# Attention scores of a graph layer: a second of seven products split again, and one list of accumulator banks

## The chip, the cores and the metric

The kernel runs on one NeuronCore of a Trainium2 chip. What counts is the time of one execution on the device, in microseconds (us). TensorE (PE in the profile) multiplies into accumulator banks of 128 x 512 fp32; VectorE (DVE) and ScalarE (ACT) copy, add and reduce; GpSimdE (POOL) and SyncE (SP) mostly issue DMA transfers.

## What is computed

Two layers of a graph network over N = 4096 nodes with 512 features, all in fp32. The second, cut to what matters here:

```python
h = x @ edge_w
e = h @ h.T                                  # 4096 x 4096 scores
e = jnp.where(adj > 0, e, NEG_BIG)
edge_att = jax.nn.softmax(e, axis=1)
output = adj * (node_att * edge_att) @ (x @ weight) + bias
x = layernorm(x + output)
```

The first layer is `layernorm(x + relu(adj @ (sign0(x) @ sign(w).T)))`. `adj` is symmetric in where it is nonzero, and `h @ h.T` is symmetric, so a tile of scores is made once and also turned (transposed) for its mirror tile.

## The kernel before

The span of the profile has five stages: the first layer's aggregation (0 to about 480 us, `acc` at L459 and L460), a short transition to 510, `h` and its like by Strassen's seven products (L101, to 602), the **score stage** (602 to 1067), and the aggregation of the second layer with its finish (L1288, then L1438, to 1909). The change lies in the score stage, and in how its buffers pass on to the aggregation.

In the score stage the 4096 x 4096 scores are cut into tiles of 512 x 512. A `Single` (L723) makes one tile by plain matmuls (`pe`, L742). A `Couple` (L766) makes two tiles side by side: rows A and columns B, B+1, that is 512 x 1024. There are twelve couples in three groups, which share their columns within a group: `couples(4, 2, 3, 0, 1)`, `couples(6, 2, 3, 0, 1, 4, 5)` and `couples(2, 0, 1)` (L1598 to L1600), with singles ahead of each group and seven after the last.

A couple is one step of the Strassen-Winograd scheme, in which a 2 x 2 block product costs seven block products (m = 0 to 6) instead of eight. `operands` (L777) prepares the left sums s1 to s4 and, once a group, the right sums t1 to t4, all on DVE. The left sums of every second couple lie in a buffer of their own (`self.sums`, L801) out of the list `free` of score slots.

- `quad(q)` (L868) makes six of the seven products for two of the four row strips (q = 0 or 1). Each product is two matmuls of 128 x 128 by 128 x 512 that follow each other in one accumulator, and the products m = 0, 5, 6, 3 go into the bank `y` one onto the other, with a copy by ScalarE after each (L902, L907, L915, L920: c11, c12, c22, c21). Products 4 and 2 go into the bank `z`: after m = 4 DVE adds z to c22 (L916), and after m = 2 it adds z to c12 (L925).
- `second` (L832) makes the product m = 1, l12 by r21, for both strips at once. It takes a further step of the same scheme: seven products of 128 x 128 by 128 x 256 (L841), added into the score strips by DVE (L844 to L863). For it `second_left` makes four sums of 128 x 128 (L826 to L829), and `second_right` four differences of 128 x 256 once a group, which lie in half a `lent` buffer (`keep`).

Each step of these functions ends in `between()`, which runs a `tick` (L579): at most one turn of a finished strip on TensorE (transposes at L704, a copy by ScalarE at L705) or the like, one or two statistics rows on DVE (L665, 0.69 us, and L666, 1.2 us for 1024 columns) and exponentials on ScalarE (L675). A row of statistics needs a mask: 512 KB of adjacency that SP loads (L650) into a free half of a `lent` buffer, if `between` finds more than two free halves. So these pieces of work stand between the products in a fixed order on each engine. A strip is written to HBM by a DMA from POOL (L895) and then released.

The main loop interleaves the parts of one couple with the second `quad` of the couple before (`rest_`): one `next` is one stretch up to a `yield`. The order on each engine is that of the program.

There are eight PSUM banks: six of the pool `ps_mm`, handed out in turn by the tile framework whenever a tile is made (`pe`, `seven`, `inner`), and two of `ps_tr` for transposes. Where a bank is taken again, the new matmul waits until the last reader of the old contents is done; so it does where a matmul writes a part of a bank of which another part is still read. After the score stage the six banks are put into a list, `banks`, which the aggregation uses.

Of the kernel before, what the change touches and what calls it, by code (L numbers as in the profile page):

```python
# [11 lines left out]
F32 = mybir.dt.float32  # L12
# [6 lines left out]
P = 128  # L19
# [10 lines left out]
def kernel(  # L30
# [13 lines left out]
    nc = tc.nc  # L44
# [3 lines left out]
    W = 512  # L48
    NG = N // W
    BG = W // P  # L50
# [515 lines left out]
    lent = [(t, t[:, : BG // 2, :], t[:, BG // 2 :, :]) for t in lent]  # L566
    free = deque(slots_p.tile([P, BG, W], F32, name=f"slot{n}") for n in range(6))
    free_h = deque(h for t in lent for h in t[1:])

    free_e = deque(pan.tile([P, W], F32, name=f"line{n}", bufs=1) for n in range(6))  # L570


    now = [0]
# [149 lines left out]
    class Single:  # L723
# [7 lines left out]
        def main(self, between):  # L731
            A, B = self.A, self.B
            s = Uses(BG + 1 if self.diag else 3 * BG)
            if self.diag:
                self.mirror.t = s
            elif self.stays:
                kept_tiles[A, B] = s.buf
            for i in range(BG):
                lo = i if self.diag else 0
                pe = ps_mm.tile([P, W], F32, name="pe", tag="mm")  # L740
                for k in range(KD):
                    nc.tensor.matmul(  # L742
                        pe[:, lo * P :],
                        hT[:, k, ts(A * BG + i, P)],
                        hT[:, k, (B * BG + lo) * P : (B + 1) * W],
                        start=(k == 0),
                        stop=(k == KD - 1),
                    )
                    if k == KD - 1 or k % 2 and not (self.diag and i > 1):
                        between()  # L750
                src = s.buf[:, i, :]
                nc.scalar.copy(src[:, lo * P :], pe[:, lo * P :])
                turns.append((now[0] + 3, lambda i=i, s=s, src=src: self.mirror.turn(s, src, i)))
                if not self.diag:
                    stats.append((self.here.ready, 1, lambda i=i, s=s, src=src: self.here.row(i, s, src)))

                    if self.stays:
                        continue

                    def store(i=i, s=s, src=src):  # L760
                        nc.gpsimd.dma_start(s_d[A][B // 2][:, i, B % 2, :], src)
                        s.used()

                    stats.append((at_once, 0, store))

    class Couple:  # L766
# [10 lines left out]
        def operands(self):  # L777
            A, B, h = self.A, self.B, KD // 2
            if B not in Couple.right:
                r11, r12 = (hT[:, :h, ts(c, W)] for c in (B, B + 1))  # L780
                r21, r22 = (hT[:, h:, ts(c, W)] for c in (B, B + 1))
                t1, t2, t3, t4 = (lopp.tile([P, h, W], F32, name="right", tag="lop") for _ in range(4))
                nc.vector.tensor_sub(t1, r12, r11)
                nc.vector.tensor_sub(t2, r22, t1)
                nc.vector.tensor_sub(t3, r22, r12)
                nc.vector.tensor_sub(t4, r21, t2)
                Couple.right[B] = r11, r21, r22, t4, t1, t2, t3
                Couple.inner_right[B] = self.second_right(r21)
            low, high = (hT[:, f : f + h, ts(A, W)].rearrange("p k (q u w) -> p k q u w", u=2, w=P) for f in (0, h))
# [6 lines left out]
            else:  # L796
                self.sums = Uses(1)
                s2, s1, s3, s4 = (
# [6 lines left out]
            self.left = l11, l12, s4, l22, s1, s2, s3  # L805
            self.inner_left = self.second_left(l12)
            self.rows11, self.written = [None] * 2, [None] * 2

# [11 lines left out]

        def second_left(self, l):

            (l11, l12), (l21, l22) = ([l[:, k, q, :] for k in range(2)] for q in range(2))
            self.inner_sums = Uses(1, free_h)
            s1, s2, s3, s4 = (self.inner_sums.buf[:, 0, ts(n, P)] for n in range(4))
            nc.vector.tensor_add(s1, l21, l22)  # L826
# [5 lines left out]
        def second(self, between):  # L832

            left, (right, keep) = self.inner_left, Couple.inner_right[self.B]
            w = W // 2
            c11, c12 = (self.rows11[0][:, c] for c in (slice(w), slice(w, W)))
            x, y = (ps_mm.tile([P, W], F32, name="inner", tag="mm") for _ in range(2))
            u, v, z = x[:, :w], y[:, :w], y[:, w:]
# [19 lines left out]
            nc.vector.tensor_add(self.rows11[0], self.rows11[0], y)  # L858
            self.written[0]()
            between()  # L860
            yield
            multiply(u, 3)
            nc.vector.tensor_add(c21, c21, u)  # L863
            self.inner_sums.used()
            keep.used()
            yield

        def quad(self, q, between):  # L868

            left, right = self.left, Couple.right[self.B]  # L870
            y, z = (ps_mm.tile([P, W], F32, name="seven", tag="mm") for _ in range(2))
            strips = [Uses(4, free_h) for _ in range(2)]
            (c11, c12), (c21, c22) = ((s.buf[:, 0, :], s.buf[:, 1, :]) for s in strips)
            self.rows11[q] = c11

# [32 lines left out]
            between()  # L908
            if q:
                yield  # L910
            multiply(z, 4, True)
# [8 lines left out]
            nc.scalar.copy(c21, y)  # L920
            between()
            if not q:
                yield
            multiply(z, 2)
            nc.vector.tensor_add(c12, c12, z)  # L925
            if q:
                written(0)
            written(1)
            between()
            yield  # L930


    banks = deque()

# [6 lines left out]
    def panel(A):  # L941
# [6 lines left out]
        yield  # L948
        pt = banks.popleft() if banks else ps_tr.tile([P, W], F32, name="ptm", tag="tr")
        for i in range(BG):  # L950
# [6 lines left out]
                stop=True,  # L957
# [6 lines left out]
        nc.scalar.copy(mrow, pt)  # L964
        if banks:
            banks.append(pt)
# [660 lines left out]
    for n, u in enumerate(runs):  # L1627
# [10 lines left out]
        quads = [[c.quad(q, between) for q in range(2)] for c in u]  # L1638
        inners = [c.second(between) for c in u]
        for k, c in enumerate(u):  # L1640
            first, second = quads[k]
            rest_ = quads[k - 1][1] if k else None
            next(first)
            if rest_:
                next(rest_)
            next(first)
            if rest_:
                next(rest_)
                if u[k - 1].sums:
                    u[k - 1].sums.used()  # L1650
# [8 lines left out]
            next(inner_)  # L1659
            next(first)  # L1660
            next(inner_)
            next(second)
            next(inner_)
            next(second)
        next(rest_ := quads[-1][1])
        next(rest_)
        if u[-1].sums:
            u[-1].sums.used()
# [5 lines left out]
    todo = deque()  # L1674
    banks.extend(ps_mm.tile([P, W], F32, name=f"bank{n}", tag="mm") for n in range(6))
    plan = deque(p for n, u in enumerate(blocks) for p in u.order(in_two(n)))
# [137 lines left out]
```

## Time and profile before

| What | us |
|---|---|
| time, median of 3 runs (lowest, highest) | 1912.76 (1912.59, 1913.26) |
| the profiled execution | 1911.35 |
| its span, first to last instruction | 1909.4 |
| score stage, 602 to 1067: PE busy | 463.5 of 465 |
| the same: DVE busy | 313.3 |
| the same: ACT busy | 314.5 |
| aggregation and finish, 1067 to 1909: PE busy | 835.3 of 842 |
| the same: DVE busy | 702.5 |

The granted TensorE clock is 0.999 over the span. An instruction's row gives its start, its length, the engine, the line, its output and inputs; a bracket after it tells how long the engine had been idle and what released it. A fp32 matmul of the program appears as two records, "x4" are thus two matmuls. Lengths of matmul records overlap those of the next, so the spacing of starts says what a matmul costs. DVE records overlap too, by about 0.08 us.

### The profile page before, as it was taken

The page shows a single profiled execution, that of the slowest core. Times are in us where ns is not written, and L with a number is a line of the kernel's source. Part 1 is how long each engine was busy: PE and PEld are TensorE (multiplying, and loading weights), DVE is VectorE, ACT ScalarE, POOL GpSimd, SP SyncE. Part 2 cuts the span into 40 slices and gives each one's busy share as a digit, 9 for nine tenths or more (in the row PEclk, how much of TensorE's full clock was granted, in tenths as well). Part 3 has the DMA queues.
Part 4 walks back from the last instruction along what each step waited for, and adds up shares of the span by engine and source line. Part 5 has one row for each costly group of instructions (what it writes and reads, how often), then busy time and mean ns, then how long its engine had stood idle before and what let it go on. Part 6 is the DMA issues. An engine that isn't in the chain of part 4 may idle for free.

```text
span 1909.4 us, 20692 instructions
## 1 busy us (share of the span) xinstructions
PE 1897.1 (99%) x6886; PEld 1234.3 (65%) x6886; DVE 1457.4 (76%) x2237; ACT 1028.8 (54%) x1653; POOL 311.3 (16%) x449
## 2 busy tenths in 40 slices
PE   9999999999999999999999999999999999999998
PEld 6888888888644555555555556666666666666646
DVE  7777677776866567686864887898879988898947
ACT  6433333333212567666767666666676567657632
POOL 0133132231421111110110111111111111110100
PEclk9999999999999999999999999999999999999999
DMA  9889899898585378577784877887777877787731
GB/s 323 300 323 359 301 347 323 326 358 307 183 305 203 125 290 320 186 257 273 293 319 155 320 288 289 287 297 286 271 280 282 293 279 275 267 313 256 283 119 56
DMA packets 143915, 520.95 MB, mean 273 GB/s; under 512 B 15040, under 2 KB 15040, under 8 KB 136128
## 3 DMA queue, kind: packets, MB, share of 16 engines
q1 hardware_dynamic: 64368, 235.43, 36.0%
q0 software_dynamic: 67632, 248.54, 34.1%
q10 hardware_dynamic: 11808, 35.66, 5.1%
q8 instruction: 54, 0.88, 0.2%
q14 instruction: 53, 0.43, 0.1%
HBM read 397.93 MB, written 121.63 MB: 272 GB/s over the span
## 4 chain that ended last, share of the span: by engine, by line
PE 88%; DVE 6%; DMA 2%; issue 1%; ACT 1%; POOL 0%; ACTq 0%; DVEq 0%; POOLq 0%
PE bank L1288 33%; PE seven L878 12%; PE acc L459 11%; PE acc L460 11%; PE pe L742 6%; PE seven L101 5%; PE po L1438 4%; PE pt L704 3%; PE inner L841 2%; DVE slot L1057 1%; PE acc L253 1%; PE acc L255 1%; PE pt L419 1%; PE pw L228 1%; DVE lent L1057 1%
## 5 line engine op out<-in xcount | busy, mean ns | idle before, releaser
L1288 PE MATMUL bank<-lent,lop 128*128 128x256 f32 (+1 forms) x1496 | 483.0, 473 | 0.1
L1288 PEld LDWEIGHTS bank<-lent,lop 128*128 128x128 f32 x1496 | 283.9, 190 | 166.9 <-issue 140.1
L459 PE MATMUL acc<-xw,hi 128*128 128x512 f32 x960 | 376.6, 392 | 0.0
L460 PE MATMUL acc<-xw,lo 128*128 128x512 f32 x960 | 374.0, 390 | 0.0
L1288 PE MATMUL bank<-slot,lop 128*128 128x512 f32 (+1 forms) x800 | 286.4, 503 | 1.0 <-DVE slot L1069 0.8
L449 ACT CAST hi<-at 128x1024 fp32r<-128x1024 f32 x120 | 126.4, 1053 | 203.0 <-PE acc L459 151.1
L1288 PEld LDWEIGHTS bank<-slot,lop 128*128 128x128 f32 x800 | 151.6, 190 | 115.4 <-issue 100.9
L1299 ACT COPY over<-bank 128x512 f32<-128x512 f32 x200 | 115.9, 585 | 201.7 <-PE bank L1288 198.1
L460 PEld LDWEIGHTS acc<-xw,lo 128*128 128x128 f32 x960 | 180.4, 188 | 36.7 <-DVE lo L451 0.2
L459 PEld LDWEIGHTS acc<-xw,hi 128*128 128x128 f32 x960 | 180.3, 188 | 36.7
L451 DVE TENSOR_TENSOR lo<-at,hi 128x1024 fp32r<-128x1024 f32 x120 | 148.2, 1235 | 65.3 <-ACT hi L449 64.9
L666 DVE CUSTOM_DVE_ANT_0 line<-lent,slot 128x512 f32<-128x512 bf16 x140 | 90.2, 686 | 55.0 <-ACT slot L705 29.0
L742 PE MATMUL pe<-hT 128*128 128x512 f32 (+3 forms) x384 | 132.1, 486 | 0.0
L675 ACT ACTIVATE line<-line,nmax_c 128x512 f32<-128x512 f32 x160 | 114.7, 722 | 21.2 <-DVE nmax_c L666 20.8
L1450 DVE SCALAR_TENSOR_TENSOR xb<-po,f,xb 128x256 f32<-128x256 f32 x84 | 40.3, 481 | 75.0 <-PE po L1438 70.8
L742 PEld LDWEIGHTS pe<-hT 128*128 128x128 f32 x384 | 64.6, 191 | 41.4 <-issue 33.8
L1057 DVE CUSTOM_DVE_ANT_1 lent<-lent,line 128x2048 f32<-128x2048 f32 x39 | 88.7, 2284 | 0.0
L1261 ACT COPY bank<-over 128x512 f32<-128x512 f32 x144 | 86.7, 603 | 0.0
L704 PEld LDWEIGHTS pt<-ident,lent 128*128 128x128 f32 x418 | 52.4, 141 | 44.8 <-issue 34.8
L1060 ACT ACTIVATE lent<-lent 128x2048 f32<-128x2048 f32 x39 | 74.9, 1920 | 8.5 <-DVE lent L1057 8.2
L705 ACT COPY slot<-pt 128x512 f32<-128x512 f32 (+3 forms) x123 | 68.3, 557 | 12.3 <-PE pt L704 12.2
L420 ACT COPY x1T<-pt 128x512 f32<-128x512 f32 x32 | 18.7, 585 | 101.9 <-PE pt L419 101.9
(302 smaller groups left out, 3075.4 us busy)
## 6 DMA issues: line engine op xcount, KB each, us to landing
lop<-lop_d SPq DMA_DIRECT2D x154, 512.0 KB, 4.9
at<-in_adj_t_dram SPq DMA_DIRECT2D x60, 1024.0 KB, 7.0
slot<-in_adj_t_dram POOLq DMA_DIRECT2D x39, 1024.0 KB, 7.9
lent<-s_d POOLq DMA_DIRECT2D x38, 1024.0 KB, 7.9
s_d<-slot POOLq DMA_DIRECT2D x30, 1024.0 KB, 8.5
lent<-in_adj_t_dram POOLq DMA_DIRECT2D x25, 1024.0 KB, 7.6
lent<-in_adj_dram SPq DMA_DIRECT2D x48, 512.0 KB, 4.8
s_d<-lent POOLq DMA_DIRECT2D x48, 512.0 KB, 6.1
```

The source lines that it names most:

```text
L101: nc.tensor.matmul(banks[bank][q], lop(m, q)[k], rop(m)[k], start=(first and k == 0), stop=(k == K - 1), skip_group_check=not first,)
L449: nc.scalar.copy(hi, aq)
L451: nc.vector.tensor_sub(lo, aq, hi.bitcast(F32))
L459: nc.tensor.matmul(acc, hi[:, c, :], xw[:, kb, :], start=(kb == 0), stop=False)
L460: nc.tensor.matmul(acc, lo[:, c, :], xw[:, kb, :], start=False, stop=(kb == NB - 1))
L675: nc.scalar.activation(line, line, AF.Exp, bias=nmax_c[:, b, c : c + 1], scale=-1.0, accum_out=sum_c[:, b, c : c + 1])
L704: nc.tensor.transpose(pt[:, j, :], src[:, ts(j, P)], ident)
L742: nc.tensor.matmul(pe[:, lo * P :], hT[:, k, ts(A * BG + i, P)], hT[:, k, (B * BG + lo) * P : (B + 1) * W], start=(k == 0), stop=(k == KD ...
L878: nc.tensor.matmul(ps, left[m][:, k, q, :], right[m][:, k, :], start=(first and k == 0), stop=(k == KD // 2 - 1), skip_group_check=not first,)
L1057: pinned[0](nc.vector._custom_dve(TENSOR_ADD_SAT, out=q, in0=q, in1=m, s0=0.0, s1=-HUGE))
L1288: nc.tensor.matmul(ps, lop[:, k, :], rop[:, k, :], start=start, stop=(k == K - 1), skip_group_check=True)
L1299: nc.scalar.copy(self.to(), self.bank[:, : self.w])
```

## The change

The product m = 2 (s4 by r22) is taken out of `quad` and made, as m = 1 is, as seven products of 128 x 256 in a new function `third`. The bank `z`, which keeps m = 4 of each quad, stays taken until `third` has put one or two of its products on top of it (`low` and `high`, the two strips' z) and DVE has added the sum to c12. Another bank, `x`, takes the rest of the products: u in its left half, z in its right one. `second_right` and `second_left` are called for both inner products; the second sums lie in the second half of the same buffer (`inner_sums`, now released by two uses), and `second_right(r22)` takes another half of `lent` per group.

The pool's rotation is replaced by a list, `banks`, of the six banks: whoever makes a tile takes the first and appends it after its last reader has been issued. The panels of the aggregation (`ptm`) take one from this list too, but for the first two row blocks. The sums of every second couple get a fixed buffer, `slot5`, out of the shared list `free`, which goes from six to five slots and gets `slot5` back at the end of the stage.

In the main loop `third` (`tail_`) of a couple runs with the couple's second `quad` during the start of the next couple; that of a group's last couple follows at once. `written[0]` (the statistics, turns and store of the strip pair with c11 and c12) moves from `second` to `third`, for both strips.

```diff
--- before.py
+++ after.py
@@ -564,11 +564,14 @@
 
     lent = [slots_p.tile([P, BG, W], F32, name=f"lent{n}") for n in range(7)]
     lent = [(t, t[:, : BG // 2, :], t[:, BG // 2 :, :]) for t in lent]
-    free = deque(slots_p.tile([P, BG, W], F32, name=f"slot{n}") for n in range(6))
+    free = deque(slots_p.tile([P, BG, W], F32, name=f"slot{n}") for n in range(5))
+    free_s = deque([slots_p.tile([P, BG, W], F32, name="slot5")])
     free_h = deque(h for t in lent for h in t[1:])
 
     free_e = deque(pan.tile([P, W], F32, name=f"line{n}", bufs=1) for n in range(6))
 
+
+    banks = deque(ps_mm.tile([P, W], F32, name=f"bank{n}", tag="mm") for n in range(6))
 
     now = [0]
     turns, stats, exps = deque(), deque(), deque()
@@ -737,7 +740,7 @@
                 kept_tiles[A, B] = s.buf
             for i in range(BG):
                 lo = i if self.diag else 0
-                pe = ps_mm.tile([P, W], F32, name="pe", tag="mm")
+                pe = banks.popleft()
                 for k in range(KD):
                     nc.tensor.matmul(
                         pe[:, lo * P :],
@@ -750,6 +753,7 @@
                         between()
                 src = s.buf[:, i, :]
                 nc.scalar.copy(src[:, lo * P :], pe[:, lo * P :])
+                banks.append(pe)
                 turns.append((now[0] + 3, lambda i=i, s=s, src=src: self.mirror.turn(s, src, i)))
                 if not self.diag:
                     stats.append((self.here.ready, 1, lambda i=i, s=s, src=src: self.here.row(i, s, src)))
@@ -785,7 +789,7 @@
                 nc.vector.tensor_sub(t3, r22, r12)
                 nc.vector.tensor_sub(t4, r21, t2)
                 Couple.right[B] = r11, r21, r22, t4, t1, t2, t3
-                Couple.inner_right[B] = self.second_right(r21)
+                Couple.inner_right[B] = self.second_right(r21), self.second_right(r22)
             low, high = (hT[:, f : f + h, ts(A, W)].rearrange("p k (q u w) -> p k q u w", u=2, w=P) for f in (0, h))
             l11, l21 = (low[:, :, :, u, :] for u in range(2))
             l12, l22 = (high[:, :, :, u, :] for u in range(2))
@@ -794,7 +798,7 @@
             if Couple.made[0] % 2:
                 s2, s1, s3, s4 = (rows.tile([P, h, 2, P], F32, name="left", tag="rows") for _ in range(4))
             else:
-                self.sums = Uses(1)
+                self.sums = Uses(1, free_s)
                 s2, s1, s3, s4 = (
                     self.sums.buf[:, n, :].rearrange("p (k q w) -> p k q w", k=h, w=P) for n in range(4)
                 )
@@ -803,8 +807,10 @@
             nc.vector.tensor_sub(s3, l11, l21)
             nc.vector.tensor_sub(s4, l12, s2)
             self.left = l11, l12, s4, l22, s1, s2, s3
-            self.inner_left = self.second_left(l12)
-            self.rows11, self.written = [None] * 2, [None] * 2
+            self.inner_sums = Uses(2, free_h)
+            self.inner_left = [self.second_left(l, n) for n, l in enumerate((l12, s4))]
+            self.rows11, self.rows12, self.zs = [None] * 2, [None] * 2, [None] * 2
+            self.written = [None] * 2
 
         def second_right(self, r):
 
@@ -818,11 +824,10 @@
             nc.vector.tensor_sub(t4, r21, t2)
             return (r11, r21, r22, t4, t1, t2, t3), keep
 
-        def second_left(self, l):
+        def second_left(self, l, n):
 
             (l11, l12), (l21, l22) = ([l[:, k, q, :] for k in range(2)] for q in range(2))
-            self.inner_sums = Uses(1, free_h)
-            s1, s2, s3, s4 = (self.inner_sums.buf[:, 0, ts(n, P)] for n in range(4))
+            s1, s2, s3, s4 = (self.inner_sums.buf[:, n, ts(m, P)] for m in range(4))
             nc.vector.tensor_add(s1, l21, l22)
             nc.vector.tensor_sub(s2, s1, l11)
             nc.vector.tensor_sub(s3, l11, l21)
@@ -831,10 +836,10 @@
 
         def second(self, between):
 
-            left, (right, keep) = self.inner_left, Couple.inner_right[self.B]
+            left, (right, keep) = self.inner_left[0], Couple.inner_right[self.B][0]
             w = W // 2
             c11, c12 = (self.rows11[0][:, c] for c in (slice(w), slice(w, W)))
-            x, y = (ps_mm.tile([P, W], F32, name="inner", tag="mm") for _ in range(2))
+            x, y = banks.popleft(), banks.popleft()
             u, v, z = x[:, :w], y[:, :w], y[:, w:]
 
             def multiply(ps, m, first=False):
@@ -856,22 +861,63 @@
             nc.vector.tensor_add(c22, c22, u)
             multiply(z, 2)
             nc.vector.tensor_add(self.rows11[0], self.rows11[0], y)
-            self.written[0]()
+            banks.append(y)
             between()
             yield
             multiply(u, 3)
             nc.vector.tensor_add(c21, c21, u)
+            banks.append(x)
             self.inner_sums.used()
             keep.used()
             yield
 
+        def third(self, between):
+
+            left, (right, keep) = self.inner_left[1], Couple.inner_right[self.B][1]
+            w = W // 2
+            (c11, c12), (c21, c22) = ((c[:, :w], c[:, w:]) for c in self.rows12)
+            x = banks.popleft()
+            u, z = x[:, :w], x[:, w:]
+
+            def multiply(ps, m, first=False):
+                nc.tensor.matmul(ps, left[m], right[m], start=first, stop=True, skip_group_check=not first)
+
+            multiply(u, 0, True)
+            nc.vector.tensor_add(c11, c11, u)
+            yield
+            low, high = self.zs
+            multiply(low[:, :w], 1)
+            multiply(low[:, w:], 2)
+            nc.vector.tensor_add(self.rows12[0], self.rows12[0], low)
+            banks.append(low)
+            between()
+            yield
+            multiply(u, 5)
+            nc.vector.tensor_add(c12, c12, u)
+            multiply(z, 4)
+            nc.vector.tensor_add(c12, c12, z)
+            nc.vector.tensor_add(c22, c22, z)
+            self.written[0]()
+            yield
+            multiply(u, 6)
+            both = self.rows12[1].rearrange("p (n w) -> p n w", w=w)
+            nc.vector.tensor_add(both, both, u.unsqueeze(1).to_broadcast([P, 2, w]))
+            multiply(high[:, :w], 3)
+            nc.vector.tensor_add(self.rows12[1], self.rows12[1], high)
+            banks.extend((x, high))
+            self.written[1]()
+            self.inner_sums.used()
+            keep.used()
+            between()
+            yield
+
         def quad(self, q, between):
 
             left, right = self.left, Couple.right[self.B]
-            y, z = (ps_mm.tile([P, W], F32, name="seven", tag="mm") for _ in range(2))
+            y = banks.popleft()
             strips = [Uses(4, free_h) for _ in range(2)]
             (c11, c12), (c21, c22) = ((s.buf[:, 0, :], s.buf[:, 1, :]) for s in strips)
-            self.rows11[q] = c11
+            self.rows11[q], self.rows12[q] = c11, c12
 
             def multiply(ps, m, first=False):
                 for k in range(KD // 2):
@@ -906,8 +952,8 @@
             multiply(y, 5)
             nc.scalar.copy(c12, y)
             between()
-            if q:
-                yield
+            yield
+            z = self.zs[q] = banks.popleft()
             multiply(z, 4, True)
             between()
             yield
@@ -918,19 +964,10 @@
             yield
             multiply(y, 3)
             nc.scalar.copy(c21, y)
-            between()
-            if not q:
-                yield
-            multiply(z, 2)
-            nc.vector.tensor_add(c12, c12, z)
-            if q:
-                written(0)
+            banks.append(y)
             written(1)
             between()
             yield
-
-
-    banks = deque()
 
 
     def lowest(A):
@@ -946,7 +983,8 @@
         nc.vector.tensor_tensor(d, nm.unsqueeze(2).to_broadcast([P, BG, NG]), nmax_c[:, cols, :], ALU.subtract)
         nc.scalar.activation(d, d, AF.Exp)
         yield
-        pt = banks.popleft() if banks else ps_tr.tile([P, W], F32, name="ptm", tag="tr")
+        own = A < 2
+        pt = ps_tr.tile([P, W], F32, name="ptm", tag="tr") if own else banks.popleft()
         for i in range(BG):
 
             nc.tensor.matmul(
@@ -962,7 +1000,7 @@
             free_e.append(panels[A - 2][1])
         mrow = take(free_e)
         nc.scalar.copy(mrow, pt)
-        if banks:
+        if not own:
             banks.append(pt)
         yield
         nc.vector.tensor_mul(d, d, sum_c[:, cols, :])
@@ -1637,15 +1675,23 @@
         final = u[-1].mirrors
         quads = [[c.quad(q, between) for q in range(2)] for c in u]
         inners = [c.second(between) for c in u]
+        tails = [c.third(between) for c in u]
         for k, c in enumerate(u):
             first, second = quads[k]
             rest_ = quads[k - 1][1] if k else None
             next(first)
             if rest_:
+                tail_ = tails[k - 1]
+                next(tail_)
                 next(rest_)
+                next(tail_)
+            next(first)
+            if rest_:
+                next(tail_)
             next(first)
             if rest_:
                 next(rest_)
+                next(tail_)
                 if u[k - 1].sums:
                     u[k - 1].sums.used()
             next(first)
@@ -1657,13 +1703,17 @@
             next(inner_)
             next(first)
             next(inner_)
-            next(first)
+            next(second)
             next(inner_)
             next(second)
             next(inner_)
-            next(second)
-        next(rest_ := quads[-1][1])
+        rest_, tail_ = quads[-1][1], tails[-1]
+        next(tail_)
         next(rest_)
+        next(tail_)
+        next(rest_)
+        next(tail_)
+        next(tail_)
         if u[-1].sums:
             u[-1].sums.used()
     while turns or stats or exps:
@@ -1672,7 +1722,8 @@
         early_.popleft()[1]()
     reclaim()
     todo = deque()
-    banks.extend(ps_mm.tile([P, W], F32, name=f"bank{n}", tag="mm") for n in range(6))
+    assert len(banks) == 6
+    free.append(free_s.popleft())
     plan = deque(p for n, u in enumerate(blocks) for p in u.order(in_two(n)))
 
 
```

## The prediction

> **What bounds the kernel now.** I read the busy table and its slices first, then the chain of waits, the waits of the score stage, the groups with shapes kept apart, the windows and last the timeline.
>
> ```profile
> span 1909.4 us, 20692 instructions
> PE 1897.1 (99%) x6886; PEld 1234.3 (65%) x6886; DVE 1457.4 (76%) x2237; ACT 1028.8 (54%) x1653; POOL 311.3 (16%) x449
> PE   9999999999999999999999999999999999999998
> DVE  7777677776866567686864887898879988898947
> ```
>
> TensorE is busy in every slice; DVE has its densest stretch in slices 19 to 24, inside the score stage (602 to 1067 us). Since ends of matmuls are modelled, I ask the waits whether TensorE is really fed there:
>
> ```profile
> PE seven L878 <- ACT lent L902: 0.8, 1, 0.8
> PE pt L704 <- ACT lent L752: 0.4, 1, 0.4
> PE seven L878 <- DVE lent L916: 0.3, 1, 0.3
> ```
>
> These are all of TensorE's waits between 602 and 1067 us: 1.5 us in 465. So each microsecond of matmul removed there ends the kernel one microsecond earlier, as long as the work that remains is still fed. What may no longer feed it is DVE, which adds the products:
>
> ```profile
> 675.90:703.00 27.10, 27.10 (x95) 14.87 (x95) 18.99 (x44) 18.57 (x41) 3.59 (x6) 1.00 0.74 279
> 918.00:932.00 14.00, 13.69 (x57) 8.21 (x56) 14.00 (x25) 8.79 (x17) 1.79 (x3) 1.00 1.00 372
> ```
>
> The columns are span, PE, PEld, DVE, ACT, POOL, clock, DMA share, GB/s. The first is one whole couple in steady state: DVE is busy 19.0 of 27.1 us. The second, where the second group of couples gives way to the third, is full: DVE 14.00 of 14 and DMA 1.00.
>
> **What the Trainium skill says.** "Perfetto Trace Analysis", Engine Utilization, gives the array 307.2 G elements/s and half of that for fp32 taken as low and high parts: an estimate of 427 ns for 128x512. The timeline agrees (four records in 1.72 us, 430 each), and a product of two such contractions has four records. "TensorE: Matmul & The Clock Gate", Step-by-step, says the next weights load while the current matmul runs; in the trace a weight load is 190 ns, which fits beside a 256-column record of 215 ns too. "PSUM — Partial Sum Buffer", PSUM bank collisions, says to guard by bank and not by address; the trace can't show that rule, but it makes a wait below. "VectorE: DVE Perf Modes", The TRN2 errata, gives (N+151)/0.96 ns for an fp32 add: 691 and 424 ns for 512 and 256; the trace has 684 and 414.
>
> **The change, part by part.** *Matmuls.* Per couple, product m=2 goes out of both `quad`s: 2 strips x 2 contractions x 2 records of 512 columns, and seven 256-column products come in, two records each. The prices:
>
> ```profile
> 683.46 0.19 PEld L878 LDWEIGHTS seven<-hT,slot 128*128 128x128 f32 x1 [0.24 <-issue]
> 684.32 1.88 PE L878 MATMUL seven<-right,left 128*128 128x512 f32 x4
> 684.52 0.69 DVE L925 TENSOR_TENSOR lent<-lent,seven 128x512 f32<-128x512 f32 x1 [3.64 <-PE seven L878]
> 686.47 0.60 PE L841 MATMUL inner<-hT 128*128 128x256 f32 x2
> 686.90 1.88 PE L878 MATMUL seven<-hT 128*128 128x512 f32 x4
> 694.67 0.59 PE L841 MATMUL inner<-lent,lent 128*128 128x256 f32 x2
> 695.10 0.59 PE L841 MATMUL inner<-hT,lent 128*128 128x256 f32 x2
> ```
>
> Starts count, not the modelled lengths: a 256-column product holds the array 0.43 us (686.47 to 686.90; 694.67 to 695.10), a 512-column record 0.43. Removed 8 x 0.43 = 3.44, added 7 x 0.43 = 3.01: gain 0.43 a couple, 5.15 over the 12 couples. Weight loads go from 8 to 14, each 0.19 under a record of 0.215. No transposes and no copies by ScalarE are added.
>
> *DVE.* Successive starts give 0.61 us for a 512-wide add (684.52 to the next at 685.12), 0.33 for 256 and 0.20 for 128 (the same lengths less 0.08 of overlap). Out go two 512-wide adds (L925), 1.22. In come four 256-wide (1.32), three 512-wide (1.83) and four 128-wide sums of `second_left(s4)` (0.80): net +2.7 per couple, and 4 x 0.33 = 1.3 per group for `second_right(r22)`; 37 us in all. The steady couple goes from 19.0 to 21.7 of 26.7, the fullest (21.4 in 836 to 863) to 24.1. That lies beside TensorE as long as no single add is late.
>
> *New waits of TensorE.* I set the order of the changed program beside these latencies: end of a matmul to DVE's start 0.20 (684.32 to 684.52), a 256-add 0.41, its end to the next matmul 0.16 (920.59 to 920.75, at the L916 wait): round trip 0.77. By ScalarE 0.20 + 0.58 + 0.15 = 0.93.
> - In `third`, z of m=4 shares a bank with u, which DVE has just read (c12 += u). One 512 contraction, 0.86, lies between: it fits if DVE is free. A steady couple's DVE queue leaves about 1.2 us before it, so nothing; where a 1.14 us mask row stands ahead, up to 1.1. Behind the waiting matmul stands all of TensorE's queue.
> - In `second`, m=5 meets c11 += u with 0.0 to 0.2 us to spare: 0.02 on average, 0.2 over nine couples.
> - The last couple of each of three groups has no next quad to put between its tail's steps. Two copies by ScalarE have 0.86 for 0.93 (0.07 each), and DVE's adds before m=4 and m=6 cost 0.1 each: 0.3 a group, 0.9 in all. From below nothing, from above one DVE row each, 1.2 x 3.
> - The head of the third group waits 0.15 for L858, in the full DVE stretch; with 2.7 + 1.3 us more in that queue the bound above is 2. The 0.3 at L916 goes, since the z that is added there has its own turn; the 0.8 at L902 stays.
> Sum of waits: 0.2 + 0.9 + 0.15 - 0.3 = 0.95.
>
> *Buffers and queues.* One list of six banks replaces rotation through the same six; every bank is appended after its last reader, and the walk through the order finds no taker closer than the waits above: nothing, at most 0.1 a couple. The slot for every second couple's sums no longer comes from the shared list, so DVE's waits for stores at L801 (2.6 and 0.8 us, hidden now) go; five shared slots instead of six could delay mirrors, whose transposes have 3 ticks or more: nothing. Halves held by the inner sums free later, so SP issues the next couple's adjacency rows (512 KB, median 4.8 us to land) only 9.4 us of TensorE time before the first use against 13 or more: hidden; under a DMA share of 1.00, where two such loads together took 10.5 (issued at 680.96), it is late by about 1 at worst in a group. At the start of the aggregates POOL blocks on a store of a slot before its first mask load and not after; in either order 5 MB follow and the last lands alike, some 7 us before its use: nothing, 1 to 3 if the store is last.
>
> Sum: 5.15 - 0.95 = 4.2 earlier. On the profiled execution 1911.35 (span 1909.4, 1.95 around it) that is 1907.15. That execution lies 1.4 under the median of 1912.76, so against the median 1908.5.
>
> **Rivals.**
> *A, the gain is half eaten by the waits (within 0.2%).* For: every new wait has 0.2 us or less to spare, and mask rows of 1.14 us on DVE come between at no fixed place. Against: DVE idles 30% in a steady couple and the same kind of chain in `second` costs TensorE nothing now. With 0.1 to 0.2 per steady couple more and tails at 0.7, waits are 0.2 + 1.3 + 2.1 + 0.3 = 4 at most, mean 2.9: 1910.5.
> *B, slower: DVE becomes the bound of the couples.* Place: the queue ahead of `third`'s c12 += u and `second`'s c11 += u. Price: one mask row (1.14 to 1.2) per couple and again at three tails. It decides from a stall of 0.43 a couple on; slower than can be told needs 5.15 + 3.83 = 9 us, 0.75 a couple. For: windows of 24 in 26.7, and a first stretch without gap. Against: most windows are 20 to 22. With 1.2 x 12 + 0.3 x 3 - 5.15: +10, 1923.
> *C, the change does less than it says.* If a short record cost more than its share, the gain per couple would go: 0.215 + 0.03 each eats 14 x 0.03 = 0.42. Against: two consecutive 256 products start exactly 0.43 apart, with different weights. 1912.8.
>
> **How the numbers follow.** What can be told from no change is about 0.2%, 3.8 us: 1908.9 to 1916.6. The forecast has 0.56 (1907 to 1909.5: 0.53 of it beyond the bound, 0.03 not); A 0.23, of which 0.02 ends just beyond the bound; B 0.18, of which 0.15 is beyond it on the other side; C 0.03. From a fuller gain than 5.15 (waits of now gone too, 1.2 us) the low end is 1906.5; the upper end reaches through A and the bounds of transition and loads to 1914.5, leaving most of B out. Added up: faster 0.55, same 0.30, slower 0.15.
>
> **What would show it.** Right: TensorE's matmul time in the score stage shorter by about 5, the first aggregate starting some 4 earlier, the list of TensorE's waits in that stage at 2 to 2.5 us, short entries from `third`'s lines behind DVE and ScalarE at the ends of the groups; the aggregates' 842 us unchanged. Wrong: waits of 0.5 or more at m=4 or m=5 in every couple (A, B); DVE busy over 25 per couple; waits for adjacency rows in DVE followed by waits of TensorE; 256-column starts further apart than 0.43 (C); a gap of TensorE at the first block's change to the second.

## The result, and the profile after

| | us |
|---|---|
| before, median of 12 runs on the same chip | 1912.49 (1910.76 to 1913.75) |
| changed, median of 12 runs | 1908.24 (1907.39 to 1909.23) |
| ratio | 0.9978, 95% interval 0.9969 to 0.9987 |
| span of the profiled execution, before and after | 1909.4, 1906.8 |

The changed kernel is 4.25 us faster; the interval of the ratio allows 2.5 to 5.9. The page of the changed kernel, its busy times and two of its rows of slices:

```profile
span 1906.8 us, 20976 instructions
PE 1893.8 (99%) x6958; PEld 1247.2 (65%) x6958; DVE 1495.8 (78%) x2357; ACT 1024.9 (54%) x1653; POOL 315.0 (17%) x449
PE   9999999999999999999999999999999999999998
DVE  7777677776876588788874887898879988898947
```

DVE has 38.4 us more to do and TensorE ends earlier. All waits of TensorE in the score stage of the changed kernel (total, times, longest):

```profile
PE bank L924 <- ACT lent L961: 0.8, 2, 0.4
PE pt L707 <- ACT slot L755: 0.4, 1, 0.4
```

The waits of 0.8 (L902) and 0.3 (L916) of before are gone from the list, and there are two new ones, at the ends of the first two groups. Line 924 is the plain product of `quad` (878 before), 883 the short one of `third`, 846 that of `second` (841 before), 961 the copy of c22 by ScalarE (915 before), 707 and 755 the transposes and a single's copy (704 and 752 before).

Two spots of the timeline decide the reading. First one steady couple of before and the same of after, from `second`'s m=0 to that of the next couple (columns span, PE, PEld, DVE, ACT, POOL, clock, DMA share, GB/s):

```profile
686.47:713.61 27.14, 27.14 (x97) 14.91 (x96) 19.70 (x47) 18.75 (x41) 3.59 (x6) 1.00 0.73 271
```

```profile
686.25:712.98 26.73, 26.73 (x103) 16.02 (x101) 23.14 (x56) 18.42 (x42) 3.97 (x6) 1.00 0.77 277
```

The period went from 27.14 to 26.73. That is 0.41, what the records cost: on average 429 ns from start to start with 512 columns and 216 with 256, so 8 x 0.429 - 14 x 0.216 = 0.41. No wait takes any of it. Second, m=5 and m=4 of `third` in that couple:

```profile
704.79 0.59 PE L883 MATMUL bank<-lent,lent 128*128 128x256 f32 x2
705.22 1.02 PE L924 MATMUL bank<-right,slot 128*128 128x512 f32 x2
705.42 0.42 DVE L896 TENSOR_TENSOR lent<-lent,bank 128x256 f32<-128x256 f32 x1 [1.11 <-PE bank L883]
706.08 0.59 PE L883 MATMUL bank<-lent,lent 128*128 128x256 f32 x2
```

By the starts m=5 ended at 705.22, and DVE's add started 0.20 later, after 1.11 us of idling; m=4 starts just when the products ahead of it are done (704.79 + 0.43 + 0.86 = 706.08), with no gap. Half a plain product stands between the two although the source has them side by side. What I wrote ahead of the prediction, that the order on each engine is that of the program, is thus not right: where no order is prescribed, the framework's scheduler sets it at build. The prediction used the built order.

From the first matmul of the first single to the first of the aggregation, the score stage took 465.04 us before (601.87 to 1066.91) and 460.57 after (602.48 to 1063.05): 4.47 less. The rest up to the end took 842.5 and 843.75. As the stage also began 0.6 later, the two profiled spans differ by 2.6 only; the profiled execution of before was 1.1 under the median of its 12 runs.

### The profile page after: what moved, and what is told of

Read it like the earlier page. It is cut to its first block, busy times and chain, and to the rows that moved or that the text cites. A ratio compares the mean times of both kernels' runs of the same rounds, so it can differ in the third digit from the quotient of the medians.

```text
span 1906.8 us, 20976 instructions
## 1 busy us (share of the span) xinstructions
PE 1893.8 (99%) x6958; PEld 1247.2 (65%) x6958; DVE 1495.8 (78%) x2357; ACT 1024.9 (54%) x1653; POOL 315.0 (17%) x449
## 4 chain that ended last, share of the span: by engine, by line
PE 67%; issue 16%; DVE 6%; POOL 5%; DMA 2%; ACT 2%; POOLq 0%; ACTq 0%; SPq 0%; DVEq 0%
PE bank L1326 33%; PE bank L924 10%; PE bank L745 6%; PE seven L101 5%; PE po L1476 4%; PE pt L707 3%; POOL mask_d L340 2%; PE bank L883 2%; PE bank L846 2%; DVE lent L1095 1%; PE acc L253 1%; PE acc L255 1%; POOL x_d L368 1%; DMA xt<-in_x_t_dram 1%; PE bank L1476 1%
## 5 line engine op out<-in xcount | busy, mean ns | idle before, releaser
L1326 PE MATMUL bank<-slot,lop 128*128 128x256 f32 (+1 forms) x1304 | 399.9, 455 | 0.8 <-DMA lop<-lop_d 0.4
L1326 PE MATMUL bank<-lent,lop 128*128 128x512 f32 (+1 forms) x992 | 369.0, 520 | 1.2 <-DVE lent L1107 1.2
L1326 PEld LDWEIGHTS bank<-slot,lop 128*128 128x128 f32 x1304 | 247.0, 190 | 129.0 <-issue 102.6
L1326 PEld LDWEIGHTS bank<-lent,lop 128*128 128x128 f32 x992 | 188.3, 190 | 154.7 <-issue 139.7
L745 PE MATMUL bank<-hT 128*128 128x512 f32 (+3 forms) x384 | 132.3, 486 | 0.0
L669 DVE CUSTOM_DVE_ANT_0 line<-lent,slot 128x512 f32<-128x512 bf16 x144 | 93.0, 687 | 40.0 <-ACT slot L755 21.7
L745 PEld LDWEIGHTS bank<-hT 128*128 128x128 f32 x384 | 64.8, 191 | 40.5 <-issue 32.5
L1095 DVE CUSTOM_DVE_ANT_1 lent<-lent,line 128x2048 f32<-128x2048 f32 x36 | 82.0, 2283 | 0.0
L1098 ACT ACTIVATE lent<-lent 128x2048 f32<-128x2048 f32 x36 | 69.2, 1921 | 19.0 <-DVE lent L1095 19.0
```

Of the source, the lines that this page charges most:

```text
L745: nc.tensor.matmul(pe[:, lo * P :], hT[:, k, ts(A * BG + i, P)], hT[:, k, (B * BG + lo) * P : (B + 1) * W], start=(k == 0), stop=(k == KD ...
L1095: pinned[0](nc.vector._custom_dve(TENSOR_ADD_SAT, out=q, in0=q, in1=m, s0=0.0, s1=-HUGE))
L1326: nc.tensor.matmul(ps, lop[:, k, :], rop[:, k, :], start=start, stop=(k == K - 1), skip_group_check=True)
```

## The experiments

The length of the score stage repeats well from profile to profile (460.57 and 460.55 for the changed kernel), so it tells tenths of a microsecond where the times, whose intervals are some +-0.08%, don't.

**The buffers without the product (e1), and its two halves (e9, e10).** The kernel before with the list of banks and the slot of its own for the sums:

```diff
-    free = deque(slots_p.tile([P, BG, W], F32, name=f"slot{n}") for n in range(6))
+    free = deque(slots_p.tile([P, BG, W], F32, name=f"slot{n}") for n in range(5))
+    free_s = deque([slots_p.tile([P, BG, W], F32, name="slot5")])
...
+    banks = deque(ps_mm.tile([P, W], F32, name=f"bank{n}", tag="mm") for n in range(6))
...
-                self.sums = Uses(1)
+                self.sums = Uses(1, free_s)
...
-            y, z = (ps_mm.tile([P, W], F32, name="seven", tag="mm") for _ in range(2))
+            y, z = banks.popleft(), banks.popleft()
...
```

> The kernel before with the change's buffers alone: the six banks from one list, the even couples' sums in a slot of their own (five shared slots), m=2 still made by plain products in quad. Theory (the gain is TensorE time of the product alone): no difference, 1912.5 us +-1, couples' period 27.1 us, DVE's waits for stores at the sums gone without effect. Rival (the buffers give part of the gain): 1909 to 1911. Rival (five slots cost something that the product pays for): 1914 or more.

Measured: 1911.0, ratio 0.9995 (0.9987 to 1.0003), the score stage 463.94 us, 1.10 less than before. The times can't tell it from no change; the trace can: of TensorE's waits the one for L916's add is gone, and that for L902's copy (L907 there) is 0.2. My theory of "no difference" falls here. The trace of before shows why; the timeline at the change from the second group to the third:

```profile
915.82 0.69 DVE L801 TENSOR_TENSOR slot<-hT 128x512 f32<-128x512 f32 x1 [0.77 <-DMA s_d<-slot]
919.91 0.68 DVE L916 TENSOR_TENSOR lent<-lent,seven 128x512 f32<-128x512 f32 x1
920.64 1.98 PE L878 MATMUL seven<-hT,slot 128*128 128x512 f32 x4 [0.31 <-DVE lent L916]
```

DVE idles 0.77 us for a store that must free the slot of the sums, at the start of the stretch where it is full; so the add of L916 ends at 920.59 and TensorE, which needs it, waits. The sum that waits for the store belongs to the third group's second couple, whose first product with these sums comes at 957; nothing needs it before, but what stands behind it in DVE's queue is held up. Two runs part the halves.

```diff
-                self.sums = Uses(1)
+                self.sums = Uses(1, free_s)
...
+    free.append(free_s.popleft())
```

> The kernel before with the sums' own slot alone (five shared slots), its banks by rotation. Theory (DVE's wait of 0.77 us for a store, at the first sum of the third group's first couple just ahead of DVE's full stretch, is what made TensorE wait there; the slot of its own takes it away): no wait of DVE for a store at the sums, TensorE's waits at L916 and L902 gone or under 0.3, score stage of 465.0 us shorter by 0.8 to 1.1. Rival (the list of banks did it): 465.0 as before, both waits there.

> The kernel before with the list of banks alone, the sums' slots out of the six shared ones. Theory of the slot: as before, 465.0 us for the score stage within 0.2, the waits of 0.3 and 0.8 there. Rival (the list did it): 463.9, the waits gone though DVE waits 0.8 for the store.

(The first of these texts speaks of the third group's first couple; it is the second, as said.) Own slot alone: 1911.45, ratio 0.9997 (0.9988 to 1.0006), stage 463.95. List alone: 1912.54, ratio 1.0001 (0.9993 to 1.001), stage 465.29, 0.25 longer than before and so just outside the 0.2 that I allowed. With the list alone both waits are still there, first of TensorE, then of DVE:

```profile
PE bank L882 <- ACT lent L906: 0.8, 1, 0.8
PE bank L882 <- DVE lent L920: 0.5, 1, 0.5
```

```profile
DVE slot L803 <- DMA s_d<-lent: 3.2, 1, 3.2
DVE slot L803 <- DMA s_d<-slot: 1.0, 1, 1.0
```

With the slot alone, DVE has no wait for a store at the sums, and of TensorE's waits there 0.2 is left. So the slot takes 1.1 us off the score stage and the list of banks nothing. In the times this 1.1 stays within the intervals.

By the starts the first wait, 0.57, is gone and the second, 1.02, is 0.51. The slot does more than end the wait for the store, though: with it one of the four sums stands behind L916's add instead of ahead of it, and the last one moves from 921 to 937, behind the full stretch, 0.6 us each. For the first wait the store's part can be read from the list alone, which leaves DVE's order there as it was: DVE waits 1.00 instead of 0.77 for the store, and TensorE stands 0.81 instead of 0.57 for the add, which is the whole 0.25 of that stage. The second wait does not follow (1.03 there). Whether the store or the moved sums make up that half of the gain, no run parts.

**Order and bank of m=4 (e3, e4).** All products of `quad`, `second` and `third`, and the first transpose of a turn, are pinned to the order of the source, so that m=4 follows m=5 at once; then the same with z in a bank of its own (the lines from u on are in e4 alone; the same pins in `second`, `third` and the turns, and the return of the new bank to the list, are left out here):

```diff
-                    nc.tensor.matmul(
+                    mm = nc.tensor.matmul(
...
+                    tc.keep_in_program_order(mm)
...
-            u, z = x[:, :w], x[:, w:]
+            u = x[:, :w]
...
-            multiply(z, 4)
+            bank = banks.popleft()
+            z = bank[:, :w]
+            multiply(z, 4, True)
```

> The changed kernel with the order of couples' products on TensorE held to that of the source, so that third's m=4 stands directly behind its m=5 in the nine couples that have a successor; u and z still share a bank. Theory (DVE's read of u has to end before z is written, and only the half product that the scheduler puts between hides it): a gap of 0.77 us (0.20 to DVE, 0.41, 0.16 back) before m=4 nine times, 6.9 us, 1915.1. Rival (DVE has time enough and the bank doesn't matter): no gap, 1908.2.

> The same held order, with z in a bank of its own. Theory (it is the sharing of the bank that makes m=4 wait): no gap at m=4, 1908.2 +-0.8, some tenths for the three heads of groups, whose order is held too. Rival (the held order itself costs, or m=4 waits for something else): as the run with the shared bank, 1914 or more.

Measured: 1922.46 with the shared bank, ratio 1.0057 (1.0044 to 1.0071), and 1917.16 with its own, 1.0029 (1.0019 to 1.0039). The shared bank in one steady couple:

```profile
680.36 0.59 PE L885 MATMUL bank<-lent,lent 128*128 128x256 f32 x2
681.47 0.70 PE L885 MATMUL bank<-lent,lent 128*128 128x256 f32 x2 [0.51 <-DVE lent L898]
```

1.11 from start to start instead of 0.43, and 0.11 more after it: 0.79 us, nine times, where 0.77 was expected. With its own bank the two stand side by side:

```profile
679.89 1.03 PE L885 MATMUL bank<-lent,lent 128*128 128x256 f32 x4
680.53 0.42 DVE L898 TENSOR_TENSOR lent<-lent,bank 128x256 f32<-128x256 f32 x1 [0.95 <-PE bank L885]
680.76 1.88 PE L928 MATMUL bank<-right,left 128*128 128x512 f32 x4
```

Four records in 0.87, no gap, while DVE reads u from 680.53 on. So the mechanism holds to 0.02 us. (The wait is one that the built program has; whether the chip would need it, no run shows.) My expectation of the times does not hold: the pinned order itself costs about 9 us (1917.16 against 1908.24), in other places, above all transposes that stand directly behind the product whose copy they turn:

```profile
PE pt L707 <- ACT lent L971: 5.8, 6, 1.2
PE bank L928 <- ACT lent L953: 2.0, 3, 0.8
```

Part of that runs beside the gap at m=4 in the other kernel (3.6 for the transposes there), so the two times differ by 5.3 and not by 7.1.

**The ends of the groups (e2, e8).** In the changed kernel, at the end of the first group:

```profile
727.21 0.20 ACT L678 ACTIVATION_READ_ACCUMULATOR line<-line,nmax_c 128x1 f32 x1
727.31 0.72 ACT L678 ACTIVATE line<-line,nmax_c 128x512 f32<-128x512 f32 x1
728.01 0.58 ACT L961 COPY lent<-bank 128x512 f32<-128x512 f32 x1
728.64 1.98 PE L924 MATMUL bank<-right,hT 128*128 128x512 f32 x4 [0.41 <-ACT lent L961]
```

m=6 ended at 727.21, so the copy could have started at 727.41; it stands behind an exponential in ScalarE's queue and starts 0.60 later. By the spacing of starts TensorE loses 0.57, and 0.10 more at the next product.

```diff
-        def third(self, between):
+        def third(self, between, last):
...
             nc.vector.tensor_add(c12, c12, u)
+            if last:
+                yield
             multiply(z, 4)
...
-        tails = [c.third(between) for c in u]
+        tails = [c.third(between, c is u[-1]) for c in u]
...
         next(tail_)
+        next(tail_)
         next(rest_)
```

> The changed kernel, in which third's product m=5 of each group's last couple stands ahead of the quad's m=3 instead of behind it, so that m=3 comes 1.29 us of TensorE time after m=6 and not 0.86. Theory (the two waits of 0.41 us for ScalarE's copy of c22 at the ends of the groups come from a copy that starts 0.6 us late, behind exponentials): both waits fall to 0.1 or less, the score stage is 0.9 us shorter, 1907.4. Rival (ScalarE's queue is what is late, and its copy slides on): the waits stay at 0.4, 1908.2.

Measured: 1906.87, ratio 0.9973 (0.9963 to 0.9982); the 0.57 is 0.13 (the 0.10 after it stays), and no wait of TensorE is listed there any more. The stage is 460.13, only 0.44 shorter and not 0.9: gaps of 0.1 to 0.3 come up elsewhere. The same kernel once more, beside the changed one on one chip:

> The version with third's m=5 ahead of the quad's m=3 at the ends of groups, on the same chip as the changed kernel: 0.9 to 1.3 us less than that, 1907. Rival (its first time was the chip's): the same time within 0.5.

Measured: 1907.01, ratio 0.9976 (0.9968 to 0.9984), against 1908.34 for the changed kernel, ratio 0.9981 (0.9975 to 0.9988). Both times it was the fastest of all, by some 1.3 us. The intervals overlap, but on the one chip 11 of its 12 runs lie below the median of the changed kernel's 21. About 0.45 of the 1.3 is in the score stage in both profiles; where the rest comes from stays open.

**The changed kernel again (e5), and DVE's room (e6, e7).**

> The changed kernel once more, beside the next three runs on one chip, to have a second profile of it. Theory: couples' period 26.72 us and no gap of TensorE at m=4 or m=5 in the steady couples again, two waits of 0.4 at ends of groups again; the aggregation's length differs from the first profile's by up to 1.5 us, since nothing in it is changed. 1908.2 +-0.8.

The period is 26.72 in every steady couple, without a gap at m=4 or m=5, and the two waits are 0.4 again. The rest after the score stage took 846.0 us in this profile against 843.75, more than the 1.5 that I allowed; the profiled execution, 1910.41, was the slowest of the 21 (median 1908.34). One wait accounts for 2.0 of the 2.3, for a load of the aggregation at 1699.5, where the DMA engines are full (share 0.99):

```profile
PE bank L1326 <- DMA lop<-lop_d: 2.4, 1, 2.4
```

At this place it was 0.4 in the first profile, 0.3 to 0.4 in e2 and e8, and isn't there before or in e1. It is there in e9 (0.4) and e10 (1.0), though, and the aggregation of e10 starts no earlier than before: an early start isn't what it takes.

```diff
+            for _ in range(2):
+                nc.vector.tensor_tensor(self.rows12[0], self.rows12[0], self.rows12[0], ALU.max)
             banks.append(low)
...
+            for _ in range(2):
+                nc.vector.tensor_tensor(self.rows12[1], self.rows12[1], self.rows12[1], ALU.max)
             banks.extend((x, high))
```

> The changed kernel with four more 512-wide DVE operations per couple in third (the maximum of a strip with itself, 4 x 0.61 = 2.4 us), two before the first between and two at the end. Theory (DVE has room: 21.7 us of 26.7 now, 24.1 then): period of a steady couple still 26.72, some waits more where DVE is full between the second and the third group, 1908.5 to 1911. Rival (DVE is about to bound the couples, as my slower case has it): 0.43 us or more per couple, 1913.5 or more.

> The same with eight such operations, 4.9 us per couple: DVE's work is 26.6 us in a period of 26.7. Theory (this is where DVE becomes the bound): queue never empties, TensorE waits in most couples, 0.5 to 2 us each, 1914 to 1930. Rival (the statistics' rows slide into the singles that follow, which leave DVE 40% idle): under 1912; then a third product of quarter size would have room too.

In e7 both loops are `range(4)`. Measured: 1909.42, ratio 0.9987 (0.9979 to 0.9996), stage 462.24, with four operations; 1913.15, ratio 1.0008 (0.9999 to 1.0016), stage 466.3, with eight. Against 460.56 that is 1.7 and 5.7 us, for 29 and 59 us of work on DVE. With four, the list of TensorE's waits shows nothing in a steady couple, but the starts do:

```profile
688.51 0.60 PE L846 MATMUL bank<-hT 128*128 128x256 f32 x2
688.95 0.60 PE L707 MATMUL pt<-ident,lent 128*128 128x128 f32 x4
689.07 0.42 DVE L849 TENSOR_TENSOR lent<-lent,bank 128x256 f32<-128x256 f32 x1
689.54 0.70 PE L846 MATMUL bank<-lent,lent 128*128 128x256 f32 x2
690.08 0.59 PE L928 MATMUL bank<-right,hT 128*128 128x512 f32 x1
```

Four transposes (x4) take 0.43, so the short product should start at 689.38 and the next at 689.81; they start 0.16 and 0.27 late, as `second`'s m=5 waits for the add to c11 (L849), before which DVE has other work. The period is 26.98, once 27.14, where `third`'s m=4 is late too. So not "still 26.72", as I expected, and not the 0.43 of the rival: it is the margin of m=5 that is used up.

With eight, 1913.15 lies between my 1914 to 1930 and the rival's 1912, and the loss is not spread evenly. By the starts TensorE stands 1.9 us between 602 and 880 (0.7 in the changed kernel), which is 0.1 to 0.2 in a steady couple and not my 0.5 to 2. It stands 5.7 us between 880 and 1000 (1.4 in the changed kernel), around the head of the third group, where DVE is busy 115 of 120 us. In the steady couples it is now `third`'s m=4 that is late, behind the add to c12 (L898):

```profile
653.26 0.42 DVE L898 TENSOR_TENSOR lent<-lent,bank 128x256 f32<-128x256 f32 x1
653.74 0.70 PE L883 MATMUL bank<-lent,lent 128*128 128x256 f32 x2
```

The added operations ahead of it hold the add back until 653.26, and the record of m=4 is 0.70 long instead of 0.59: 0.1 lost inside the record.

## Why the prediction was right, point by point

The direction held, and so did the mechanism: TensorE time of the product, at full price in the steady couples, less some waits at the ends of the groups. That 1908.5 was forecast and 1908.24 measured says less than it seems: the gain of 4.25 is known to 2.5 to 5.9 us only, and two terms of the sum were off in opposite directions. The score stage, which repeats to hundredths, shows the terms. In the order of the prediction:

- *The waits of now, 1.5 us*: the list leaves out what lies inside a record and gaps that are too short for it. By the starts they are 2.2.
- *Matmuls, 0.43 a couple, 5.15 in all*: right but for 0.02 a couple: 27.14 to 26.73, 4.9 in all. The rival that short products cost more than their share (C) is nearly out: 216 ns for half of 429 is 1.5 ns a record, not the 30 that it needs. The 427 ns that the prediction works out fit one record; a whole fp32 matmul of 128x512 is two of them, 0.86 us, as the prediction priced it.
- *DVE, 37 us more*: 38.4. In the steady couple it became 23.1 of 26.7, more than the 21.7 forecast. Before, couples differed (18.3 to 22.1), as their sums were made now in one and now in the next; the 19.0 was one window, and the couple shown had 19.7. The nine operations that it has more take 3.4 by the lengths of their records, where the 2.7 was by spacing. The number of statistics rows is the same.
- *m=4 in steady couples, nothing*: right, and DVE's idling ahead of it, 1.11, is about the 1.2 that I had forecast. The step was tested by taking the cover away: without the half product between, 0.79 for the forecast round trip of 0.77, and 0 with a bank of its own.
- *m=5, 0.2 in all*: 0 here; that the room is small is real, since 2.4 us more of DVE turn it into a gap of 0.27.
- *Ends of groups, 0.9*: mis-sized. 0.67 for each of the first two and 0.36 for the last, 1.7. I counted a copy by ScalarE as prompt (0.93 for 0.86 of cover); it stands behind an exponential and starts 0.60 late. DVE's adds, for which I had most of the sum, are not among the listed waits; by the starts 0.1 of theirs shows, at the last group.
- *Head of the third group, 0.15; L916's 0.3 goes; L902's 0.8 stays*: the last is wrong, and the second came true for a reason other than mine: not because z has its own turn, for it goes with the slot alone, without the product. Before, the gaps there were 1.6 by the starts, after 0.3. What failed is the line on buffers: "DVE's waits for stores at L801 (2.6 and 0.8 us, hidden now) go", at a price of nothing. The second of them was not hidden: it held DVE up at the start of its full stretch, and TensorE stood for it at L916's add. The slot alone, which also moves sums in DVE's order, brings 1.1 us.
- *The list of banks, nothing; loads of adjacency rows hidden*: right. The list alone gives 465.3 for 465.0, and DVE has no wait for an adjacency row. What I did not foresee are six new waits of DVE for stores, at the first of the inner sums (L831), 0.3 to 0.6 us each; they cost TensorE nothing in the steady couples, where they lie.
- *The aggregation unchanged*: no run shows a change. 843.75 and 846.0 us against 842.5, with waits for a load at one place; in all profiles of these kernels, e3 and e4 apart, it lies between 842.5 and 846.0, and in e9 and e10, which leave it as it was but for the buffers, at 843.6 and 843.7. The two profiles of the changed kernel alone differ by 2.25, so the 1.25 between the first two profiles says nothing; what makes the load late stays open.

Together: the stage gained 4.9 from the product and lost 0.5 to waits (2.7 by the starts after, 2.2 before), where 5.15 and 0.95 were forecast. The waits came out near the forecast since two errors offset each other: 1.1 from the slot, where nothing was counted, and about 0.8 more at the ends of groups. That is luck.

The slower rival (B, DVE as the bound) did not come in any couple at its price, a stall of 1.14 to 1.2 us: with 2.4 us more on DVE a steady couple loses 0.27, with 4.9 it loses 0.1 to 0.2, and most of the loss is around the head of the third group. Its places were right: `second`'s add to c11 in the first of these runs, `third`'s add to c12 in the second. (Its sum takes 0.3 for each of the three ends of groups, though its text has a mask row of 1.2 there: it should read +13 and not +10.) Only with about 4.9 us more of DVE per couple is the kernel back at the time of before (1913.15 for about 1912).

## What to carry to other kernels

Where one engine is fed without a gap, price a change by the spacing of starts on it, and then look for the few places where another engine's answer has less cover than its round trip, with its queue at that moment and not with the operation alone. Idling on an engine that is not the bound can cost nothing in one place, as DVE's 2.6 us at L801 did before, and its full length in another, as just ahead of the stretch where DVE is full: 0.23 us more there (e10) were 0.24 more on TensorE. A wait that stays out of the list of waits can still be read from a start that comes later than the products ahead of it account for.

## What the runs showed of the hardware that I had not expected

The round trip from TensorE through an add of 256 columns on DVE and back repeated nine times at 0.78 to 0.79 us. With DVE busy 25.65 us of the 26.73 from 686.25 to 712.98 in e7, TensorE's records leave no gap in that stretch, and by the starts it lost only 0.15 us.
